# k and v of the later pairs by the seven-product scheme at two levels, q ahead of them, and the attention scale in Wo

## The chip, the core and the metric

The kernel runs on one core of one Trainium2 chip. The core has TensorE (PE, matrix products into PSUM), VectorE (DVE), ScalarE (ACT), GpSimd (POOL) and SyncE (SP), whose queue issues the transfers. Each engine works through its own instructions in a fixed order; a waiting instruction holds up those behind it. The metric is the device time of one execution in microseconds (us).

## The reference, cut to what matters

All tensors are float32. There are 8 sequences of 512 tokens with 512 features.

```python
xn = layernorm(x)                                  # x: (8, 512, 512)
q, k, v = xn @ Wq.T + bq, xn @ Wk.T + bk, xn @ Wv.T + bv
phi_q, phi_k = elu(q) + 1, elu(k) + 1
context = phi_q * cumsum(phi_k * v, axis=tokens) * 32 ** -0.5
s = context @ Wo.T + bo
h = fwht(xn * SU_ug) / 64                          # feed-forward branch, 512 -> 2048 -> 512
a = silu(h @ W_gate.T * w_gate) * (h @ W_up.T * w_up)
d = fwht(a * SU_dp) / 64 @ W_down.T * w_down
out = x + s * silu(d)
```

## The kernel before

**Seven products.** Every matrix product is cut into 2 x 2 blocks and made from seven block products in place of eight. `P1, P2, P7, P3, P4, P5, P6` name the seven factors and their places in a tile. The factors of weights and tokens are sums and differences of blocks (`encode_weights`, `encode_tokens`). A product accumulates in PSUM: bank `px` is read as it grows (after P1, P6, P5 and P3), so each next product into it waits for the reading of the one before; `py` and `pz` hold the others. There are three `px` banks, one `py` and two `pz`, so the next block product starts while the last is still read out.

**Pairs.** Sequences are worked in pairs, `p` = 0 to 3. The token tile `xo` holds 7 outer factors (blocks of sequence and half of the features) by 7 inner ones (again blocks, inside each). `inner_tokens` and `inner_t3` make the inner factors on VectorE. The inner place P7 first holds a plain block and is overwritten by `inner_t3` once the plain blocks are no longer read.

**Two kinds of product.** `group` (line 460 in the helper) applies the scheme once: 7 products of two matrix multiplications of 128x128 by 128x512. `attention` calls it through `project` for k, v and q, twice each (`g`). `block_product` (line 638) is one outer factor of the scheme applied twice: 7 inner products, each two multiplications (the two lanes, gate and up) of 128x128 by 128x256. `hidden_unit` calls it for the 7 outer factors (`outer`) and sums their results on the way: factors P1 and P5 start from nothing and are read out mostly by ScalarE; the other five add an earlier tile, and all seven readings of theirs are on VectorE. Of hidden units there are four per pair (`u`). Pair 0 does its first three by `group` (gate, up), since the weights for the second level have yet to be made.

**Attention.** For each `g`, `attention` makes k, v and q; `elu_plus_one` uses ScalarE twice (Relu, Exp) and VectorE once (line 712); VectorE multiplies v by phi_k (L724), sums over tokens with a scan (L729), and multiplies by phi_q and the scale into the context tile `co` (L737). GpSimd then makes the other factors of `co` (L304 to L307). `project_out` multiplies `co` by Wo after the first hidden unit.

**Weights.** In pair 0 the weights are loaded raw, encoded and stored in DRAM (`keep_w`); `inner_w` makes second-level factors of gate and up from them. Later pairs load stored factors, one tile of 896 KB for each `get_w`, up to three tiles ahead (`ask(3)`, four buffers in `wpool`).

**Order.** `at(place, fn)` puts a step into an agenda whose unit is about one product of two short multiplications; `later(us, fn)` puts work into a queue that `pace` takes out after a reading, up to a given number of microseconds. `background` lowers the priority of what is issued in it. The order on each engine is then fixed ahead of the run by a scheduler.

## Time and profile before

| | |
|---|---|
| timed runs (three) | 1553.84, 1555.47, 1557.9 us; median 1555.47 |
| span of the profiled execution | 1552.4 us (no device time of its own is recorded for it; the median lies 3.1 us above) |
| PE busy | 1523.8 us (98%) |
| PE weight loads busy | 1121.3 us (72%) |
| DVE busy | 1002.4 us (65%) |
| ACT busy | 418.9 us (27%) |
| POOL busy | 436.7 us (28%) |
| moved by DMA | 273.31 MB, 176 GB/s over the span |
| granted PE clock | 0.998 |

"Busy" is the share of the span in which the engine executes something. A matrix multiplication in float32 appears as two records of one half each, so 128 records of a `px` group of k are 64 multiplications. Records of PE are pipelined: the time of one is the distance to the next, not its own length. The profile's page says that spans on GpSimd are rough. In the timeline a row is: start, length, engine, line, operation, output and inputs, count, and in brackets the idle time before it with what ended it.

### The profile page before, as it was taken

The numbers are of one execution on the slowest core, as the hardware profiler recorded it, in microseconds if no ns is written. First come the engines' busy times: TensorE is split into PE (matmuls) and PEld (weight loads), VectorE is DVE, ScalarE is ACT, GpSimd is POOL, SyncE is SP. The second block draws the span as 40 slices with busy tenths as digits, with TensorE's granted clock in tenths as the row PEclk, the third lists the DMA queues.
The fourth block names the chain that finished last, engine by engine and source line by source line (L and its number), as shares of the span: only waits on it lengthen the run. The fifth ranks groups of instructions, "written<-read, shape, count | busy, mean of one in ns | idle before, by whom it ended". The sixth has DMA issues, their size and how long they took to land.

```text
span 1552.4 us, 15693 instructions
## 1 busy us (share of the span) xinstructions
PE 1523.8 (98%) x5924; PEld 1121.3 (72%) x5924; DVE 1002.4 (65%) x1423; ACT 418.9 (27%) x664; POOL 436.7 (28%) x236
## 2 busy tenths in 40 slices
PE   7989999999999999999999999999999999999998
PEld 3436446746874588888884488888886478888887
DVE  7989787378867665516767674715675575533673
ACT  4452341141125411112114431111213431111211
POOL 1232233004320261205511144302621126210631
PEclk9999999999999999999999999999999999999999
DMA  8345877687985244354576344335574233535462
GB/s 276 98 141 176 258 250 240 214 276 261 267 283 162 90 154 160 95 166 164 166 265 235 93 143 149 114 119 186 175 245 155 87 112 102 191 100 174 164 258 81
DMA packets 197692, 273.31 MB, mean 176 GB/s; under 512 B 56816, under 2 KB 155120, under 8 KB 193392
## 3 DMA queue, kind: packets, MB, share of 16 engines
q1 hardware_dynamic: 197472, 272.27, 54.0%
q8 instruction: 47, 0.77, 0.2%
q14 instruction: 29, 0.24, 0.0%
q10 hardware_dynamic: 144, 0.03, 0.0%
HBM read 196.25 MB, written 76.02 MB: 175 GB/s over the span
## 4 chain that ended last, share of the span: by engine, by line
PE 90%; DVE 6%; DMA 1%; ACT 1%; issue 1%; SPq 0%; POOL 0%; POOLq 0%; DVEq 0%; ACTq 0%
PE px_gu L638 20%; PE px_dn L536 13%; PE pz_gu L638 10%; PE pz_dn L536 6%; PE py_gu L638 5%; PE px_k L460 4%; PE py_dn L536 4%; PE px_o L536 3%; PE px_v L460 3%; PE px_q L460 3%; PE px_up L460 2%; PE pz_o L536 2%; PE pz_k L460 2%; PE pz_v L460 2%; PE pz_q L460 2%; PE px_gate L460 1%
## 5 line engine op out<-in xcount | busy, mean ns | idle before, releaser
L638 PE MATMUL px_gu<-xo,w_gu 128*128 128x256 f32 x1456 | 347.7, 380 | 1.4 <-DVE sb_gu L648 1.4
L638 PEld LDWEIGHTS px_gu<-xo,w_gu 128*128 128x128 f32 x1456 | 275.7, 190 | 45.9 <-issue 5.0
L536 PE MATMUL px_dn<-w_down,ho 128*128 128x256 f32 x1024 | 228.7, 379 | 0.0
L536 PEld LDWEIGHTS px_dn<-w_down,ho 128*128 128x128 f32 x1024 | 194.6, 190 | 28.6 <-issue 2.4
L638 PE MATMUL pz_gu<-xo,w_gu 128*128 128x256 f32 x728 | 187.7, 380 | 1.1 <-DVE u L476 1.1
L838 POOL TENSOR_TENSOR u<-u,v 128x1024 f32<-128x1024 f32 x26 | 61.0, 2367 | 365.9 <-DVE u L676 347.4
L638 PEld LDWEIGHTS pz_gu<-xo,w_gu 128*128 128x128 f32 x728 | 137.5, 190 | 22.3 <-DVE u L476 1.5
L536 PE MATMUL pz_dn<-w_down,ho 128*128 128x256 f32 x496 | 112.5, 379 | 1.7 <-DVE u L476 1.7
L536 PEld LDWEIGHTS pz_dn<-w_down,ho 128*128 128x128 f32 x496 | 93.7, 190 | 16.4 <-DVE u L476 2.1
L638 PE MATMUL py_gu<-xo,w_gu 128*128 128x256 f32 x364 | 93.4, 379 | 0.0
L304 POOL TENSOR_TENSOR co<-co 128x512 f32<-128x512 f32 x8 | 14.6, 1829 | 266.3 <-DVE co L737 266.3
L883 POOL TENSOR_TENSOR s<-s,d 128x512 f32<-128x512 f32 x30 | 40.0, 1333 | 165.4 <-ACT d L882 165.4
L638 PEld LDWEIGHTS py_gu<-xo,w_gu 128*128 128x128 f32 x364 | 69.2, 190 | 9.4
L842 POOL TENSOR_TENSOR v<-v,r 128x1024 f32<-128x1024 f32 x26 | 60.9, 2361 | 26.9 <-DVE r L676 26.9
L460 PE MATMUL px_k<-xo,w_k 128*128 128x512 f32 x128 | 61.8, 606 | 0.0
L460 PE MATMUL px_v<-xo,w_v 128*128 128x512 f32 x128 | 60.6, 594 | 0.0
L460 PE MATMUL px_q<-xo,w_q 128*128 128x512 f32 x128 | 60.3, 592 | 0.0
L828 ACT ACTIVATE a<-a,cols_sb 128x512 f32<-128x512 f32 x26 | 18.7, 721 | 149.5 <-DVE a L676 147.8
L882 ACT ACTIVATE d<-d 128x512 f32<-128x512 f32 x31 | 19.5, 630 | 144.4 <-DVE d L551 124.7
L536 PE MATMUL px_o<-w_o,co 128*128 128x256 f32 x256 | 58.2, 379 | 0.0
L828 ACT ACTIVATE u<-u,cols_sb 128x512 f32<-128x512 f32 x52 | 36.9, 720 | 78.2 <-DVE u L676 75.0
L536 PE MATMUL py_dn<-w_down,ho 128*128 128x256 f32 x256 | 57.9, 379 | 0.0
(269 smaller groups left out, 2417.4 us busy)
## 6 DMA issues: line engine op xcount, KB each, us to landing
w_gu<-d_gu SPq DMA_DIRECT2D x91, 896.0 KB, 4.5
w_down<-d_down SPq DMA_DIRECT2D x56, 512.0 KB, 3.8
d_s<-o SPq DMA_DIRECT2D x8, 1024.0 KB, 5.7
d_d<-dn SPq DMA_DIRECT2D x8, 1024.0 KB, 7.7
d<-d_d SPq DMA_DIRECT2D x8, 1024.0 KB, 6.3
s<-d_s SPq DMA_DIRECT2D x8, 1024.0 KB, 8.1
y<-in_x_dram SPq DMA_DIRECT2D x8, 1024.0 KB, 6.4
out_dram<-y SPq DMA_DIRECT2D x15, 512.0 KB, 3.2
```

The lines of the kernel that those rows point to most:

```text
L304: eng.tensor_tensor(o[..., P5, :], o[..., P7, :], o[..., P1, :], ALU.subtract)
L460: nc.tensor.matmul(p.rearrange("p a t -> p (a t)") if len(r.shape) == 2 else p, ws[k][:, i, :], r, start=(first and k == 0), stop=(k == n ...
L536: nc.tensor.matmul(p[:, c], t[:, (2 * g + c) * P : (2 * g + c + 1) * P], ws[i](k), start=(first and k == 0 and c == cs[0]), stop=(k == n - ...
L638: nc.tensor.matmul(p[:, lane], w[:, lane, i, :], x[:, i, :], start=(first and lane == 0), stop=True, skip_group_check=True,)
L828: nc.scalar.activation(g[:, m], g[:, m], AF.Silu, scale=col("w_gate", u + m * NU + a * NG))
L838: nc.gpsimd.tensor_tensor(r[:, m], ru1[:, m], rv[:, m], ALU.add)
L842: nc.gpsimd.tensor_tensor(rv[:, m], rv[:, m], rr[:, m], ALU.add)
L882: nc.scalar.activation(d, d, AF.Silu)
L883: (nc.vector if final and (a, s) == (1, 0) else nc.gpsimd).tensor_tensor(r, r, d, ALU.mult)
```

## The change

Pair 0 is kept, save for the scale. In pairs 1 to 3, `attention_by_blocks` takes the place of `attention`. It first makes q by `group` for both `g`, and writes phi_q into the places P1, P2, P7 and P3 of `co`. It then overwrites the inner P7 blocks (`inner_t3`, which came after all of attention) and makes k and v together as the two lanes of `by_blocks`, which is `hidden_unit`'s sequence of outer factors with what follows taken out as `got`. For each of the four output blocks, `heads` adds the biases and takes the Relu and Exp on ScalarE, ends phi_k on VectorE (`positive`, two of 128x512), multiplies v by phi_k on GpSimd (`weighted`), scans on VectorE (`scan`, two of 128x512), multiplies into `co` on GpSimd (`context`), and makes the other factors of `co` on GpSimd (`sub`). The VectorE steps among them are inserted after readings by `pace`, with 0.9 as its allowance, during k and v and the first hidden unit.

In pair 0, `plain_kv` stores the plain factors of Wk and Wv, and `factors_kv`, hung on the ends of groups 11 to 14, loads the encoded weights again, makes the four second-level factors on VectorE, and stores them. The attention scale goes from L737 into the raw blocks of Wo, multiplied on ScalarE before they are encoded. The later pairs load two tiles for q and seven for k and v, where they loaded six.

```diff
+        elif name[0] == "kv":
+            nc.sync.dma_start(w, inner["kv"][:, name[1]])
...
+    def plain_kv(m, g, w):
+        if "kv" not in inner:
+            inner["kv"] = dram.tile([P, 7, 2, 7, P], F32, tag="d_kv", name="d_kv")
+        d = inner["kv"][:, :, ("k", "v").index(m)]
+        for c, j in ((P1, 0), (P2, 1)) if g == 0 else ((P4, 1),):
+            nc.sync.dma_start(d[:, :, c, :], w[:, j])
+    def factors_kv(m, lo, hi):
+        n = hi - lo
+        t = t8.tile([P, 4, 4, P], F32, tag="t", name=f"f_{m}_{lo}")
+        for g in range(2):
+            nc.sync.dma_start(
+                t[:, 2 * g : 2 * g + 2, :n],
+                kept[f"{m}_{g}"].rearrange("p (j s e) -> p j s e", j=2, s=7)[:, :, lo:hi],
+            )
+        d = inner["kv"][:, lo:hi, ("k", "v").index(m)]
+        def made(c, o, x, y, op):
+            nc.vector.tensor_tensor(t[:, o, :n], t[:, x, :n], t[:, y, :n], op)
+            nc.sync.dma_start(d[:, :, c, :], t[:, o, :n])
+        def make():
+            for c, o, x, y, op in (
+                (P5, 3, 2, 3, ALU.add), (P7, 2, 0, 2, ALU.subtract),
+                (P6, 0, 3, 0, ALU.subtract), (P3, 1, 1, 0, ALU.subtract),
+            ):
+                with background():
+                    made(c, o, x, y, op)
+        at(8, make)
...
-                nc.vector.tensor_tensor(s, px, add[:, m, :, q], ALU.add)
+                pace(nc.vector.tensor_tensor(s, px, add[:, m, :, q], ALU.add), time)
             return s
+        def output(o, s, p):
+            pace(nc.vector.tensor_tensor(o, s, p, ALU.add), time)
...
+    def elu_plus_one(r, name, to=None):
+        neg = t8.tile([P, 2, 2, L], F32, tag="t", name=f"neg_{name}")
+        for h in range(2):
+            nc.scalar.activation(neg[:, h], r[:, h], AF.Relu, scale=-1.0)
+            nc.scalar.activation(neg[:, h], neg[:, h], AF.Exp, scale=-1.0)
+            nc.vector.scalar_tensor_tensor(
+                r[:, h] if to is None else to(h), r[:, h], 1.0, neg[:, h], ALU.add, ALU.max
+            )
...
-                    nc.vector.scalar_tensor_tensor(
-                        co[:, g, h : h + 3 : 2, :], k[:, h], QSCALE, q[:, h], ALU.mult, ALU.mult
-                    )
+                    nc.vector.tensor_tensor(co[:, g, h : h + 3 : 2, :], k[:, h], q[:, h], ALU.mult)
...
+    def attention_by_blocks(p, xo, co, get_w):
+        for g in range(2):
+            def with_q(q, g=g):
+                elu_plus_one(q, f"q_{p}_{g}", lambda h: co[:, g, h : h + 3 : 2, :])
+            project(p, "q", g, xo, get_w, with_q)
+        catch_up()
+        inner_t3(xo, (P1, P5, P6, P2, P7))
+        at(9, lambda: inner_t3(xo, (P3, P4)))
+        made = []
+        def sub(c, a, b):
+            nc.gpsimd.tensor_tensor(co[:, :, c], co[:, :, a], co[:, :, b], ALU.subtract)
+        def heads(t, a, s):
+            k, v = (t[:, :, lane].rearrange("p m q t -> p m (q t)") for lane in range(2))
+            place = (P1, P7, P2, P3)[2 * a + s]
+            neg = co[:, :, (P4, P6, P4, P5)[2 * a + s]]
+            for m in range(2):
+                nc.scalar.activation(
+                    neg[:, m], k[:, m], AF.Relu, bias=nbk[:, m + 2 * a : m + 2 * a + 1], scale=-1.0
+                )
+            nc.scalar.activation(neg, neg, AF.Exp, scale=-1.0)
+            for m in range(2):
+                nc.scalar.activation(v[:, m], v[:, m], AF.Identity, bias=col("bv", m + 2 * a))
+            def positive(m):
+                nc.vector.scalar_tensor_tensor(
+                    k[:, m], k[:, m], bk1[:, m + 2 * a : m + 2 * a + 1], neg[:, m], ALU.add, ALU.max
+                )
+            def scan(m):
+                nc.vector.tensor_tensor_scan(
+                    k[:, m], ones.to_broadcast([P, L]), v[:, m], 0.0, ALU.mult, ALU.add
+                )
+            def weighted():
+                nc.gpsimd.tensor_tensor(v, v, k, ALU.mult)
+                at(4, summed)
+            def summed():
+                for m in range(2):
+                    later(1.2, scan, m)
+                later(0.0, context)
+            def context():
+                nc.gpsimd.tensor_tensor(co[:, :, place], co[:, :, place], k, ALU.mult)
+                made.append(place)
+                if place == P7:
+                    sub(P5, P7, P1)
+                    sub(P6, P3, P5)
+                    sub(P7, P3, P7)
+                if place == P2:
+                    sub(P4, P2, P6)
+            def first():
+                for m in range(2):
+                    later(0.6, positive, m)
+                later(0.0, weighted)
+            at(5, first)
+        by_blocks(p, "kv", xo, lambda i: get_w("kv", i), heads, 0.9)
+        def finish():
+            while len(made) < 4:
+                if not idle and not urgent:
+                    advance(1)
+                catch_up()
+        return finish
...
-    def hidden_unit(p, u, xo, ho, get_w, last):
+    def by_blocks(p, name, xo, weights, got, time=0):
...
-            gated(rv, 1, 1, nc.gpsimd)
+            got(rv, 1, 1)
...
-        outer(P2, ra, ra, lambda: gated(ra, 0, 0, nc.gpsimd))
+        outer(P2, ra, ra, lambda: got(ra, 0, 0))
...
+        outer(P3, rest["u3"], rest["u3"], lambda: got(rest["u3"], 0, 1))
+        outer(P4, ru1, rr, lambda: got(ru1, 1, 0))
+    def hidden_unit(p, u, xo, ho, get_w, last, time=0):
...
+        by_blocks(p, f"gu_{u}", xo, lambda i: get_w("gu", (u, i)), gated, time)
...
+            if m == "o":
+                for raw in (w[:, P1 : P7 + 1], w[:, P4]):
+                    nc.scalar.mul(raw, raw, QSCALE)
             encode_weights(eng, w)
             keep_w(name, t)
+            if m in ("k", "v"):
+                plain_kv(m, g, w)
...
-        queue += [(p, m, g) for g in range(2) for m in ("k", "v", "q")]
+        if p == 0:
+            queue += [(p, m, g) for g in range(2) for m in ("k", "v", "q")]
+        else:
+            queue += [(p, "q", g) for g in range(2)]
+            queue += [(p, "kv", i) for i in (P1, P5, P6, P2, P7, P3, P4)]
...
+    nc.vector.tensor_scalar(nbk, col("bk", 0, KD), -1.0, None, ALU.mult)
+    nc.vector.tensor_scalar(bk1, col("bk", 0, KD), 1.0, None, ALU.add)
...
+    for n, m, lo, hi in ((11, "k", 0, 4), (12, "k", 4, 7), (13, "v", 0, 4), (14, "v", 4, 7)):
+        plan.setdefault(n, []).append(lambda m=m, lo=lo, hi=hi: factors_kv(m, lo, hi))
...
-        attention(p, xo, co, get_w)
-        if p:
-            catch_up()
-            inner_t3(xo, (P1, P5, P6, P2, P7))
-            at(9, lambda: inner_t3(xo, (P3, P4)))
+        heads_made = (attention_by_blocks if p else attention)(p, xo, co, get_w)
...
-                hidden_unit(p, u, xo, ho, get_w, u % 2 == 1)
+                hidden_unit(p, u, xo, ho, get_w, u % 2 == 1, 0.9 if u == 0 else 0)
                 if u == 0:
+                    heads_made()
                     project_out(p, co, get_w)
```

## The prediction

> **What bounds the kernel now.** I read the page's first part, the chain that ended last, and the windows by stage; then the timeline of single engines at the places that the change touches.

> ```profile
> span 1552.4 us, 15693 instructions
> PE 1523.8 (98%) x5924; PEld 1121.3 (72%) x5924; DVE 1002.4 (65%) x1423; ACT 418.9 (27%) x664; POOL 436.7 (28%) x236
> PE 90%; DVE 6%; DMA 1%; ACT 1%; issue 1%; SPq 0%; POOL 0%; POOLq 0%; DVEq 0%; ACTq 0%
> ```

> TensorE carries 90% of the chain. Windows show where it idles: columns are PE, PEld, DVE, ACT and POOL busy, clock, DMA share, GB/s.

> ```profile
> 240.00:260.00 20.00, 18.29 (x70) 13.01 (x69) 15.21 (x19) 1.17 (x2) 10.31 (x5) 1.00 0.68 200
> 457.00:530.00 73.00, 73.00 (x178) 33.07 (x177) 49.56 (x64) 32.91 (x41) 7.11 (x6) 1.00 0.50 155
> 530.00:572.00 42.00, 42.00 (x190) 35.57 (x189) 30.86 (x44) 14.11 (x19) 20.48 (x11) 1.00 0.43 138
> ```

> The second is attention of pair 1, the third its first hidden unit: TensorE is never idle. Only work taken off TensorE, or a new wait of TensorE, moves the time there. The idle time lies in pair 0 and at both ends. The next rows, TensorE's timeline at 522 us, give the price of a product: the distance between starts, since lengths overlap.

> ```profile
> 522.67 1.88 PE L460 MATMUL pz_q<-xo,w_q 128*128 128x512 f32 x4
> 524.39 1.88 PE L460 MATMUL px_q<-xo,w_q 128*128 128x512 f32 x4
> 526.11 1.03 PE L638 MATMUL px_gu<-xo,w_gu 128*128 128x256 f32 x4
> 526.97 1.03 PE L638 MATMUL py_gu<-xo,w_gu 128*128 128x256 f32 x4
> ```

> A product of two multiplications (four records) costs 1.717 us 512 wide and 0.863 us 256 wide.

> **TensorE.** Removed per later pair: k and v, four groups of 7 products, 28 x 1.717 = 48.1 us. Added: 7 outer factors of 7 products, 49 x 0.863 = 42.3 us. That is 5.8 us less, 17.4 us for three pairs. Weight loads double for the same columns but stay covered: 190 ns each beside 216 ns between starts, and hidden units already run so.

> **VectorE in the same stretch.** The prices are starts of neighbouring readings (541.49, 542.09), 0.60 us for 128x512; half of the 128x1024 row of L712, 0.60, for one `positive`; half of the two scans in 2.33, 1.16, for a `scan`. Before, k and v of a pair took 12 readings (7.2), twelve operations of 128x1024 at 1.14 (13.7) and 8 scans (9.3): 30.2 us beside 48.1 of TensorE. After: 41 readings (24.6), 8 `positive` (4.8), 8 scans (9.3): 38.7 beside 42.3. The total fits, but not evenly. A block is done only after outer factors P2, P7, P3 and P4, so all 16 inserted operations come late. In the order that the scheduler fixes for the changed kernel they lie between the first readings of outer P3 and the sixth product of the hidden unit's fourth outer factor. There are 34 readings (20.4) and 16 insertions (14.1) there, 34.5 us, against 42 products, 36.2 us. VectorE is 95% booked before it waits for anything.

> **What it waits for.** GpSimd gets 16 operations of 128x1024 per pair (rows of L838, L829: 2.36 us each) where `co` had 8 of 128x512 (1.27): +27.6 us. Some 10 of them fall in that stretch, 25 us of about 42, busy some 60%. These rows show what becomes of two engines that both read SBUF:

> ```profile
> 69.07 5.93 POOL L305 TENSOR_TENSOR co<-co 128x512 f32<-128x512 f32 x1
> 74.97 1.72 POOL L307 TENSOR_TENSOR co<-co 128x512 f32<-128x512 f32 x1
> 74.39 1.17 DVE L939 TENSOR_TENSOR r_gate<-r_gate 128x512 f32<-128x512 f32 x1
> 75.48 1.76 DVE L940 TENSOR_TENSOR r_gate<-r_gate 128x512 f32<-128x512 f32 x1
> 537.69 2.19 POOL L304 TENSOR_TENSOR co<-co 128x512 f32<-128x512 f32 x1 [28.34 <-DVE co L737]
> 539.26 1.70 DVE L737 SCALAR_TENSOR_TENSOR co<-k,q 128x1024 f32<-128x1024 f32 x1
> 98.00 6.01 DVE L729 TENSOR_TENSOR_SCAN k<-ones,v 128x512 f32<-128x512 f32 x4
> 563.64 4.69 POOL L842 TENSOR_TENSOR v<-v,r 128x1024 f32<-128x1024 f32 x2 [2.13 <-DVE r L676]
> 565.40 0.69 DVE L648 TENSOR_TENSOR sc_gu<-px_gu,u 128x512 f32<-128x512 f32 x1 [0.17 <-PE px_gu L638]
> ```

> L305 needed 5.93 us in place of 1.27 while VectorE went through SBUF operations without a gap. L940 needed 1.76 in place of 0.68: it stood until L307 ended at 76.69. The multiplication at 539.26 took 1.70, not 1.22, and GpSimd's operation ended 0.62 after it began. Four scans beside GpSimd took 6.01 us, not 4.66. But a reading out of PSUM (565.40) keeps its 0.69 beside GpSimd. So hidden units did not pay; `positive` and `scan`, inserted where GpSimd runs, will, and readings queued behind them stand too. TensorE waits for these, since the next product into `px` needs the last reading.

> On the price: 16 insertions, 60% of them meeting a running operation, with half of 2.36 left of it: 16 x 0.6 x 1.18 = 11.3 us. VectorE then needs 34.5 + 11.3 = 45.8 us in 36.2, 9.6 short. TensorE tolerates some lag: around 539 us VectorE ran two inserted multiplications (1.22 and 1.70) and TensorE lost some 0.3. I allow 2, which leaves about 7.6.

> [...]

> **ScalarE's queue.** `heads` puts instructions that wait for GpSimd ahead of readings. Count from when the last product of outer P7 has been issued. VectorE has its result 1.6 us later; GpSimd, which started `weighted` of the block before at 0.4 and ends it at 2.8, makes its two sums until 7.5. ScalarE's second Relu of that block starts then. Behind it come a bias, the Exp, and Relu and bias of the next block: 4 x 0.57 (starts of neighbours at 480.64 and 481.21) and 0.97 (474.27 and 475.24), to 10.8. Only then does it read the hidden unit's first `px`, to 11.4. TensorE wants that bank ten products later, at 8.6. It loses 2.8 us, whatever the lock does; part of VectorE's lag is worked off meanwhile. I take 8 us per pair for both. The bounds: 1 (insertions fall into gaps, ScalarE's wait is met by other products) and 12 (strict turns).

> Old stalls that go: a later pair lasted 363.2 us (820.2 less 457.1, first products of k) against 361.9 of products; 0.3 lies at the old handover to the hidden unit, 0.9 in three pairs. `inner_t3` moves ahead of k and v with the same seven operations (0.42 us) and the same wait, for the end of q: nothing. ScalarE's table loads stay as many (23; 1.28 us each where uncovered). Multiplying by phi_q without the scale is one input's arithmetic less: nothing.

> **Pair 0.** 16 operations of VectorE (0.60 or less, 9 us), in windows from 220 to 300 us with 34 us of VectorE idle: hidden there. Transfers: 6 stores of 448 KB early, then 8 loads and 16 stores, 7.2 MB. At 295 GB/s, the most that the window 180 to 200 us moved with all engines busy, that is 24 us; in 200 to 300 us the DMA share leaves 27 idle. It just fits. SP's queue is in order, so stores that wait for VectorE stand ahead of the raw loads of gate and of `w_down`, and at 240 to 260 us TensorE already lost 1.7 with a weight load as releaser. Bounds 0 and 10, nearest to that row: 2. Weights of later pairs: +2.7 MB each at 6 us per tile of 896 KB, the pace of hidden units, whose transfers land in 4.5: nothing. Scaling Wo is four ScalarE operations off the chain: nothing.

> **Sum.** -17.4 + 3 x 8 - 0.9 + 2 = +7.7 us. The span becomes 1560.1; the median lies 3.1 above the span, so 1563.2.

> **The rivals.**
> *The insertions mostly find gaps (faster).* VectorE's readings come every 0.863 us and take 0.60, GpSimd may slip between them, and the lag is absorbed; ScalarE's 2.8 us stay, with 0.4 more: -17.4 + 9.6 - 0.9 + 2 = -6.7, 1548.8. For it: TensorE lost only 0.3 at 539 us. Against: 60% of GpSimd's time is taken. It decides below 3.8 us of loss per pair.
> *Full gain.* ScalarE's wait is covered too, 0.5 us per pair: -14.8, 1540.7. Against it stands the order of its queue.
> *Break-even.* Loss of 3.8 to 7 us per pair: 1550.6 to 1560.2; at 5.4, 1555.4.
> *Pair 0 pays more.* Loads come late behind the added transfers, 10 in place of 2: 1571.2.

> **How the numbers follow.** A measurement here can tell about 0.3%, 4.7 us, from no change. Forecast (loss over 7 us per pair) 0.45; pair 0 besides 0.12; break-even 0.18; insertions in gaps 0.17; full gain 0.08. Slower is 0.45 + 0.12, rounded 0.57; same 0.18; faster 0.25. The range leaves out the full gain and the upper half of the case with pair 0: 1546 to 1576, where 12 us per pair gives 1575. The likeliest case alone is 1560 to 1576.

> **What would show it.** Right: per pair, TensorE's products last 5.8 us less, but the first products of two successive pairs stand about 365 us apart, not 363; TensorE waits at the start of the first hidden unit for ScalarE's `sa_gu` and VectorE's readings; scans show means well above 1.16 us, and GpSimd's `co` products above 2.36. Wrong: pairs of 358 to 360 us, scans at 1.16, no wait at that handover. A TensorE idle time between 200 and 400 us that grows by more than 5 us would put the loss in pair 0.

## The result, and the profile after

The changed kernel takes 1599.98 us, the median of four runs (1593.7 to 1602.12), against 1554.65 for the kernel before beside it: a ratio of 1.0285, 95% interval 1.0261 to 1.0309. It is slower, by 45 us, outside the range that was given. The profiled execution is the fastest of the four (1593.7, span 1591.9).

The page of the changed kernel, its first part and the chain:

```profile
span 1591.9 us, 16438 instructions
PE 1526.9 (96%) x6176; PEld 1176.0 (74%) x6176; DVE 1064.3 (67%) x1516; ACT 419.1 (26%) x680; POOL 525.0 (33%) x260
PE 69%; DVE 5%; issue 2%; DMA 2%; POOL 1%; SPq 1%; ACT 1%; POOLq 0%; DVEq 0%; ACTq 0%
```

TensorE's share of the chain falls from 90% to 69%. Its busy time has not fallen although its products are shorter, largely because some ran at half clock, as shown below.

Where the time went is read from landmarks on TensorE's timeline, the first product of each pair. In the profiled execution pair 1 begins at 469.78 us (before 457.07), pair 2 at 841.81 (820.23). So pair 0 lost 12.7 us, where 2 were predicted, and a later pair takes 372.0 us, where 363.2 were taken and 365 predicted.

Pair 1 by windows (after the length, the columns as before: PE, PEld, DVE, ACT, POOL, clock, DMA share, GB/s). The first window holds q and most of k and v, the second their end and the first hidden unit:

```profile
470.00:534.00 64.00, 64.00 (x241) 45.28 (x240) 49.39 (x74) 26.59 (x36) 12.05 (x7) 1.00 0.65 204
534.00:592.00 58.00, 48.40 (x201) 39.45 (x200) 48.51 (x58) 19.03 (x28) 42.68 (x18) 0.94 0.37 116
```

All of the 9.6 us that TensorE idles in pair 1 lie in the second, beside VectorE at 84% and GpSimd at 74%. Four of its waits there, from TensorE's timeline:

```profile
540.42 0.70 PE L676 MATMUL px_gu<-xo,w_gu 128*128 128x256 f32 x2 [3.58 <-ACT sa_gu L684]
...
557.55 1.99 PE L676 MATMUL px_gu<-xo,w_gu 128*128 128x256 f32 x8 [1.26 <-DVE sa_gu L686]
561.10 1.13 PE L676 MATMUL pz_gu<-xo,w_gu 128*128 128x256 f32 x4 [1.55 <-DVE v_gu L690]
569.56 2.07 PE L676 MATMUL px_gu<-xo,w_gu 128*128 128x256 f32 x4 [2.09 <-DVE sc_gu L686]
```

The first is the forecast wait for ScalarE's reading; the others are VectorE's lag. The timelines of ScalarE, GpSimd and VectorE ahead of it:

```profile
533.16 0.72 ACT L811 ACTIVATE co<-v_kv,nbk 128x512 f32<-128x512 f32 x1 [7.89 <-POOL v_kv L943]
539.81 0.56 ACT L684 COPY sa_gu<-px_gu 128x512 f32<-128x512 f32 x1
528.45 2.36 POOL L829 TENSOR_TENSOR a_kv<-a_kv 128x1024 f32<-128x1024 f32 x1 [7.87 <-DVE a_kv L819]
530.76 5.60 POOL L943 TENSOR_TENSOR v_kv<-v_kv,r_kv 128x1024 f32<-128x1024 f32 x2
537.59 2.35 POOL L838 TENSOR_TENSOR co<-co,a_kv 128x1024 f32<-128x1024 f32 x1 [1.23 <-DVE a_kv L824]
531.80 2.41 DVE L824 TENSOR_TENSOR_SCAN a_kv<-ones,a_kv 128x512 f32<-128x512 f32 x1
534.71 2.73 DVE L824 TENSOR_TENSOR_SCAN a_kv<-ones,a_kv 128x512 f32<-128x512 f32 x1
538.78 2.38 DVE L819 SCALAR_TENSOR_TENSOR v_kv<-v_kv,bk,co 128x512 f32<-128x512 f32 x2 [0.75 <-ACT co L814]
```

ScalarE stands 7.89 us for GpSimd's sums (L943), which stand behind `weighted` (L829). VectorE's scans, inserted into the same stretch, take 2.41 and 2.73 us, not 1.16, and two `positive` 2.38, not 1.20, each beside one of GpSimd's operations from 528.45 to 536.36 and from 537.59 to 539.94 us. All this is as the prediction had it. What it had not is in the next rows, windows of 2 us after the first wait:

```profile
540.00:542.00 2.00, 0.89 (x3) 0.49 (x4) 2.00 (x4) 0.58 (x2) 0.70 (x1) 1.00 0.00 0
542.00:544.00 2.00, 2.00 (x6) 1.55 (x6) 1.55 (x3) 2.00 (x3) 1.67 (x1) 0.52 0.00 0
```

The clock column falls to 0.52 once the wait is over. TensorE is busy all of 542 to 544 us, but with 6 records where 9 or 10 fit at 0.216 us each. The clock records of this trace hold six such stretches in the three later pairs, 23.9 us in all at half clock, so up to 12 us of work lost, 4 per pair. The kernel before has none there. What sets them off is worked out in the last section.

### The profile page after: what moved, and what is told of

Read it like the earlier page. It is cut to its first block, busy times and chain, and to the rows that moved or that the text cites. A ratio compares the mean times of both kernels' runs of the same rounds, so it can differ in the third digit from the quotient of the medians.

```text
span 1591.9 us, 16438 instructions
## 1 busy us (share of the span) xinstructions
PE 1526.9 (96%) x6176; PEld 1176.0 (74%) x6176; DVE 1064.3 (67%) x1516; ACT 419.1 (26%) x680; POOL 525.0 (33%) x260
## 4 chain that ended last, share of the span: by engine, by line
PE 69%; DVE 5%; issue 2%; DMA 2%; POOL 1%; SPq 1%; ACT 1%; POOLq 0%; DVEq 0%; ACTq 0%
PE px_gu L676 17%; PE px_dn L574 11%; PE pz_gu L676 9%; PE pz_dn L574 5%; PE py_gu L676 4%; PE px_kv L676 4%; PE py_dn L574 3%; PE px_o L574 3%; PE px_q L498 3%; PE pz_kv L676 2%; PE pz_o L574 1%; PE pz_q L498 1%; SPq L237 1%; POOL v_kv L943 1%; PE py_kv L676 1%
## 5 line engine op out<-in xcount | busy, mean ns | idle before, releaser
L676 PE MATMUL px_gu<-xo,w_gu 128*128 128x256 f32 x1456 | 354.8, 384 | 24.1 <-ACT sa_gu L684 10.7
L676 PEld LDWEIGHTS px_gu<-xo,w_gu 128*128 128x128 f32 x1456 | 277.4, 192 | 71.0 <-ACT sa_gu L684 11.9
L676 PE MATMUL pz_gu<-xo,w_gu 128*128 128x256 f32 x728 | 192.3, 388 | 7.3 <-DVE v_gu L690 4.7
L939 POOL TENSOR_TENSOR u_gu<-u_gu,v_gu 128x1024 f32<-128x1024 f32 x26 | 61.0, 2369 | 347.1 <-DVE u_gu L717 334.4
L676 PEld LDWEIGHTS pz_gu<-xo,w_gu 128*128 128x128 f32 x728 | 140.2, 194 | 31.0 <-DVE v_gu L690 6.1
L676 PE MATMUL py_gu<-xo,w_gu 128*128 128x256 f32 x364 | 93.4, 379 | 0.0
L676 PE MATMUL px_kv<-xo,w_kv 128*128 128x256 f32 x336 | 82.5, 386 | 0.1
L676 PEld LDWEIGHTS py_gu<-xo,w_gu 128*128 128x128 f32 x364 | 69.2, 190 | 9.4
L676 PEld LDWEIGHTS px_kv<-xo,w_kv 128*128 128x128 f32 x336 | 65.2, 195 | 14.6 <-issue 3.6
L943 POOL TENSOR_TENSOR v_gu<-v_gu,r_gu 128x1024 f32<-128x1024 f32 x26 | 60.9, 2363 | 20.6 <-DVE r_gu L717 20.4
L915 POOL TENSOR_TENSOR ho<-g,u 128x512 f32<-128x512 f32 x6 | 12.9, 2152 | 153.6 <-DVE u L514 153.6
L966 ACT ACTIVATE a_gu<-a_gu,cols_sb 128x512 f32<-128x512 f32 x26 | 18.7, 721 | 169.4 <-DVE a_gu L717 167.8
L966 ACT ACTIVATE u_gu<-u_gu,cols_sb 128x512 f32<-128x512 f32 x52 | 36.9, 720 | 78.2 <-DVE u_gu L717 75.0
```

Of the source, the lines that this page charges most:

```text
L676: nc.tensor.matmul(p[:, lane], w[:, lane, i, :], x[:, i, :], start=(first and lane == 0), stop=True, skip_group_check=True,)
L915: nc.gpsimd.tensor_tensor(ho[:, P1], g[:, 0, 0], r[:, 0, 0], ALU.mult)
L939: nc.gpsimd.tensor_tensor(r[:, m], ru1[:, m], rv[:, m], ALU.add)
L943: nc.gpsimd.tensor_tensor(rv[:, m], rv[:, m], rr[:, m], ALU.add)
L966: nc.scalar.activation(g[:, m], g[:, m], AF.Silu, scale=col("w_gate", u + m * NU + a * NG))
```

## The experiments

Beside each the kernel before ran on the same chip, and a difference to it is to its median there. That median lay between 1553.77 and 1556.44, so a difference between two versions that ran on different chips is uncertain by some 3 us. "Per pair" is the distance between the first products of pairs 1 and 2 in the profile.

### Pair 0 alone, later pairs alone

`pair0_only`: the changed kernel with the old attention in all pairs, so that the new weights are made and not read; Wo is still scaled.

```diff
-            queue += [(p, "q", g) for g in range(2)]
-            queue += [(p, "kv", i) for i in (P1, P5, P6, P2, P7, P3, P4)]
...
+        queue += [(p, m, g) for g in range(2) for m in ("k", "v", "q")]
...
-        heads_made = (attention_by_blocks if p else attention)(p, xo, co, get_w)
+        attention(p, xo, co, get_w)
```

> The kernel before with the additions of pair 0 alone: its weights' extra factors are made and stored, and nothing reads them; q, k and v of all pairs are computed as before. By the traces the first product of pair 1 comes 12.7 us later than before in the changed kernel. Theory (the transfers of pair 0 and their place in SP's queue cost that): about 1567 us, 12.7 above the kernel before, pairs 363.2 us apart, the loss between 220 and 450 us with a DMA share near 0.9. Rival (pair 0 lost most of that to chance, a slow clock after a wait that the kernel before has too): 1555 to 1559.

Measured: 1570.79, 15.5 above before, ratio 1.0101 (1.0086 to 1.0116). Pair 1 starts at 474.3 us, pairs are 363.3 apart. So pair 0 alone costs 15 us.

`later_only`: the changed kernel without `plain_kv` and `factors_kv`; the later pairs load stored factors of gate and up for k and v, which have other values by it.

```diff
-            nc.sync.dma_start(w, inner["kv"][:, name[1]])
+            nc.sync.dma_start(w, inner[0][:, name[1]])
...
-            if m in ("k", "v"):
-                plain_kv(m, g, w)
...
```

> The changed kernel without the additions of pair 0; the later pairs take the gate and up factors of hidden unit 0 as weights of k and v, so k and v have other values, with the same instructions and bytes. Theory (the two losses add up): 12.7 us less than the changed kernel, about 1587, pairs 372 us apart. Rival (the loss in the later pairs hangs on a late arrival out of pair 0): below 1575.

Measured: 1595.79, only 4 below the changed kernel. Pairs are 372.7 apart, but pair 1 starts at 471.2 us: pair 0 loses 14 us although no factor is made. Both expectations fail, and the theory that the transfers cost pair 0 its time falls with them. Two suspects were left in pair 0: the scaling of Wo, and whatever else the change leaves there.

A chain through three queues spoke for Wo. The DMA queue of the kernel before, then that of `later_only` with VectorE and TensorE:

```profile
118.65 0.33 SPq L326 DMA_DIRECT2D d_o<-w_o  x1
130.53 6.89 SPq L354 DMA_DIRECT2D w_up<-in_wup_t_dram  x8
```

```profile
128.29 0.33 SPq L328 DMA_DIRECT2D d_o<-w_o  x1
133.19 5.44 SPq L358 DMA_DIRECT2D w_up<-in_wup_t_dram  x8
139.78 0.69 DVE L1049 TENSOR_TENSOR r_up<-w_up 128x512 f32<-128x512 f32 x1 [3.50 <-DMA w_up<-in_wup_t_dram]
141.72 3.62 PE L574 MATMUL pz_o<-w_o,co 128*128 128x256 f32 x8 [3.45 <-DVE g L514]
```

GpSimd encodes Wo only when ScalarE has scaled it, and by then the context's subtractions stand in front. The store of Wo is issued 9.6 us later, the loads of `w_up` behind it 2.7 us later, VectorE waits 3.5 us for them, and an unrelated reading behind that wait holds TensorE.

### The parts of pair 0

`wo_scale_only` is the kernel before with this alone (and the scale taken out of the product with phi_q):

```diff
+            if m == "o":
+                for raw in (w[:, P1 : P7 + 1], w[:, P4]):
+                    nc.scalar.mul(raw, raw, QSCALE)
```

> The kernel before with one part of the change: Wo is scaled by ScalarE when it is loaded, and the product with phi_q carries no scale. No factors for k and v are made. The runs so far lose 12 to 17 us in pair 0 with and without those factors, and in all of them GpSimd encodes the second Wo tile only after the context's eight subtractions, since it waits for ScalarE's scaling: the tile's store then stands 10 us longer in SP's queue, and the raw loads of w_up behind it come 2.7 us late, on which VectorE waits 3.5 us and TensorE 3.5. Theory (the scaling, through two queues, is most of the loss in pair 0): first product of pair 1 at 466 to 471 us in place of 457.1; 1564 to 1570. Rival (the extra transfers and tiles are the loss): 1554 to 1558.

Measured: 1558.49, 2.8 above before, ratio 1.0020 (1.0010 to 1.0031). The chain is there (TensorE waits 3.3 us for g), but it is worth 3 us, not 10. (Its profile, in which pair 1 starts at 464.2 us, is of the slowest of its ten runs.)

`factors_only` is the kernel before with `plain_kv` and `factors_kv` called as in the change.

> The kernel before with the other part of pair 0's additions alone: the factors of k and v are made and stored (7.2 MB, 16 operations of VectorE) and not read; the scale stays in the product with phi_q, Wo is as before. Theory (scaling of Wo is most of the loss): 1555 to 1562, first product of pair 1 at 458 to 463 us, no wait of 3.5 us for g near 141 us. Rival (the transfers are the loss): 1566 to 1572.

Measured: 1557.39, 1.7 above before, ratio 1.0013 (1.0001 to 1.0025). The added transfers, 10.1 MB in all (283.40 against 273.31; the prediction's 7.2 and its six early stores), cost the 2 us that the prediction gave them.

`v_scaled` is the changed kernel with the scale in ScalarE's bias addition, for which it keeps a scaled bias in one more constant tile:

```diff
+    bvq = const.tile([P, KD], F32, tag="bvq", name="bvq")
...
-                nc.scalar.activation(v[:, m], v[:, m], AF.Identity, bias=col("bv", m + 2 * a))
+                nc.scalar.activation(
+                    v[:, m], v[:, m], AF.Identity, bias=bvq[:, m + 2 * a : m + 2 * a + 1], scale=QSCALE
+                )
...
```

> The changed kernel with the scale of attention in another place: in pair 0 in the product with phi_q as before, in the later pairs in ScalarE's addition of the bias to v (an activation that is there anyway), and not in Wo. Theory (the scaling of Wo costs pair 0 some 8 to 12 us through the queues of GpSimd and SP): 1588 to 1593, later pairs unchanged at 372 us. Rival (pair 0 loses to the transfers): 1598 to 1602.

Measured: 1600.01, no gain. The parts sum to 4.5 us, and whole versions lose 12 to 17. The only thing left that the losing kernels have and these two parts lack is a pair of constant tiles of 16 bytes per partition, `nbk` and `bk1`; `v_scaled` has a third, `bvq`, so it was no clean test of Wo's scaling.

`before_shifted` adds only these to the kernel before:

```diff
+    nbk = const.tile([P, KD], F32, tag="nbk", name="nbk")
+    bk1 = const.tile([P, KD], F32, tag="bk1", name="bk1")
     su_dp = const.tile([P, NF], F32, tag="su_dp", name="su_dp")
...
+    nc.vector.tensor_scalar(nbk, col("bk", 0, KD), -1.0, None, ALU.mult)
+    nc.vector.tensor_scalar(bk1, col("bk", 0, KD), 1.0, None, ALU.add)
```

> The kernel before with nothing of the change but two small constant tiles (nbk and bk1, 128x4 each) and the two operations that fill them; nothing reads them. They stand ahead of all large tiles, so every large SBUF tile lies 64 bytes further: xo at byte 20032 of its partition, not 19968 (a multiple of 512), and the rest with it. Every run so far with these two tiles lost 12 to 17 us in pair 0 (with the factors, without them, with and without the scaling of Wo); the two without them lost 2 to 3. In the former the mean packet of 128 bytes took 17 to 20 us in the trace's units against 13.0 in the latter. Theory (the place of the tiles slows the transfers of pair 0): 1563 to 1570, first product of pair 1 at 465 to 473 us, 13.0 becomes 16 to 20. Rival (chance of the order in pair 0; the tiles don't matter): 1554 to 1558.

Measured: 1565.87, 12.1 above before, ratio 1.0079 (1.0064 to 1.0094); pair 1 starts at 466.7 us. `after_aligned` is the test from the other side, the changed kernel with the two tiles in the last pool:

```diff
-    nbk = const.tile([P, KD], F32, tag="nbk", name="nbk")
-    bk1 = const.tile([P, KD], F32, tag="bk1", name="bk1")
...
+    nbk = small.tile([P, KD], F32, tag="nbk", bufs=1, name="nbk")
+    bk1 = small.tile([P, KD], F32, tag="bk1", bufs=1, name="bk1")
```

> The changed kernel with nbk and bk1 at the end of SBUF, so that all large tiles lie where they lie in the kernel before. Same instructions. Theory (the shift by 64 bytes costs pair 0 some 9 us): 1588 to 1593, first product of pair 1 at 459 to 464 us, later pairs 372 us apart. Rival (it doesn't matter): 1598 to 1602.

Measured: 1588.27, 11.7 below the changed kernel (10.8 when each is held against its own kernel before); pair 1 starts at 464.6 us, pairs are 372.2 apart. Same instructions, another address. Which transfers feel it is seen in the list of DMA issues (count, KB each, median us to landing), first of the kernel before, then of `before_shifted`, then of `after_aligned`:

```profile
z<-d_x SPq DMA_DIRECT2D x24, 256.0 KB, 4.7
```

```profile
z<-d_x SPq DMA_DIRECT2D x24, 256.0 KB, 6.1
```

```profile
z<-d_x SPq DMA_DIRECT2D x24, 256.0 KB, 5.2
```

`z` is loaded in packets of 128 bytes. Their mean duration is 13.0 or 13.1 ns in each run whose tiles lie where they did before and 16.4 to 19.6 in each run with the tiles in front. It is a part of them that is slow: in `before_shifted` 28% take more than 13 ns, in the kernel before 0.2%. The raw loads of gate go from 2.9 to 3.7 us in `before_shifted`, and VectorE's waits for raw gate and up weights from 5.5 to 12.9 us in all. That the place of the tiles makes the 12 us is shown; by what step inside the transfers is not.

How the loads reach TensorE shows in pair 0, first of the kernel before, then of `before_shifted`:

```profile
0.00:457.07 457.07, 434.22 (x1388) 262.17 (x1389) 362.30 (x538) 152.71 (x287) 119.69 (x81) 1.00 0.71 226
0.00:466.71 466.71, 440.56 (x1389) 266.23 (x1390) 357.03 (x540) 153.10 (x287) 121.94 (x81) 0.98 0.72 221
```

Of the 9.6 us between these two profiles 3.3 are more idle time of TensorE and 6.3 are longer busy time for the same products: it ran at half clock for 20.5 us, against 3.4 before. All four runs of `before_shifted` show a granted clock of 0.992 to 0.994, the kernel before beside them 0.997 or more, which is some 6 us.

`aligned_v_scaled` takes the scale out of Wo as `v_scaled` did, at the old addresses.

> As the last, and the scale of attention goes into ScalarE's bias addition of v (later pairs) and the product with phi_q (pair 0) in place of Wo, which costs no instruction. Theory (scaling Wo holds up GpSimd's and SP's queues for some 3 us): 1585 to 1590, 3 less than the run beside it. Rival (nothing): the same as the run beside it.

Measured: 1584.91, 3.4 less than `after_aligned`, as expected. This is the base of the experiments that follow; its pairs are 373.4 us apart.

### The later pairs

`products_on_vector` was made on the changed kernel itself:

```diff
-                nc.gpsimd.tensor_tensor(v, v, k, ALU.mult)
+                nc.vector.tensor_tensor(v, v, k, ALU.mult)
...
-                nc.gpsimd.tensor_tensor(co[:, :, place], co[:, :, place], k, ALU.mult)
+                nc.vector.tensor_tensor(co[:, :, place], co[:, :, place], k, ALU.mult)
```

> The changed kernel with the two products of each block (phi_k times v, and the prefix sum times phi_q) on VectorE in place of GpSimd, as inserted operations of 1.2 us. VectorE gets 9 us more per pair, GpSimd 19 less. [...]

Measured: 1599.61, the same as the changed kernel. The mean of the scans falls (by group from 2.20, 2.57 and 1.21 us to 1.21, 1.96 and 1.21), but the 9 us of added work cost as much as that gained. The time lies between the author's two estimates: 1577 to 1592 with scans of 1.2 to 1.8 us, 1610 to 1627 with the 9 us on top.

`products_left_out` leaves both lines out.

> The changed kernel without the two products of each block: v isn't weighted by phi_k, and the context keeps phi_q alone. VectorE has the same work as in the changed kernel, GpSimd 8 operations of 2.36 us less per pair. Theory (the turns with GpSimd and ScalarE's queue behind GpSimd's sums are the loss): scans near 1.2 to 1.8 us, a later pair loses 2 to 6 us in place of 14.7: 1562 to 1575. Rival (VectorE's own 34.5 us in 36.2 are too many, whatever GpSimd does): 1593 to 1600.

Measured: 1578.47; 366.6 us per pair, and no half clock in the later pairs. By the profiles 5.4 of the 14.7 us go, by the times (21.5 us less) some 7 per pair, a little outside the expected range. That is not the turns alone: TensorE's wait for `sa_gu` falls with them from 3.58 to 1.55 us.

`hold_removed` puts ScalarE's steps of one block later:

```diff
+            def on_scalar():
...
-            at(5, first)
+            if (a, s) == (1, 1):
+                at(9, on_scalar)
+            else:
+                on_scalar()
```

> The changed kernel with ScalarE's five instructions for the block that waits for GpSimd's sums (Relu, Relu, Exp and the two biases of v) put into its queue nine products later, and what follows them with them; the reading sa_gu of the first hidden unit no longer stands behind them. Nothing else differs. Theory: the wait of 3.6 us for sa_gu goes and with it the half clock that follows it (1.7 us), while VectorE's lag is the next wait: 2 to 4 us less per pair, 1588 to 1594. Rival (VectorE is late anyway and the wait only changes its name): 1598 to 1602.

Measured: 1618.29, 18 worse. It was not the clean cut that the expectation claims: the block now comes after its successor, so two differences of the context tile are taken before it is finished and hold other values, and GpSimd's subtractions meet VectorE's last insertions. The timelines of GpSimd and VectorE there:

```profile
564.68 8.64 POOL L804 TENSOR_TENSOR co<-co 128x1024 f32<-128x1024 f32 x3
562.68 5.22 DVE L822 SCALAR_TENSOR_TENSOR u_kv<-u_kv,bk,co 128x512 f32<-128x512 f32 x2
```

Two `positive`, 1.40 us when alone, take 5.22 beside them, and TensorE waits 7.0 us for a reading behind. As a test of the hold it is inconclusive.

`kv_first` computes k and v ahead of q, so that the insertions should fall into the 24 us of q ("the last" in its expectation is `aligned_v_scaled`). For that the products with phi_q move from GpSimd to VectorE, and `inner_t3` runs seven operations more per pair. Its edit, of which this is the order alone:

```diff
...
-            queue += [(p, "q", g) for g in range(2)]
             queue += [(p, "kv", i) for i in (P1, P5, P6, P2, P7, P3, P4)]
+            queue += [(p, "q", g) for g in range(2)]
```

> The last, with k and v computed ahead of q in the later pairs, so that the block-wise operations that VectorE has inserted (positive, scan) fall into the 24 us of q, in which it has only 8 us of its own, and not into the first hidden unit; the reading of the first hidden unit no longer stands behind ScalarE's steps for the blocks. The scans write into the context tile, phi_q is multiplied in afterwards on VectorE as in the kernel before. The inner sums of the tokens are made in the down product of the pair before; place P7 of them is turned back for q and again for the hidden units (7 more operations of 0.4 us). Theory (the place of the inserted work is the loss): a later pair takes 357 to 361 us, 1545 to 1556 in all. Rival (VectorE is overloaded wherever it falls): 368 to 372 us per pair, 1580 to 1590.

Measured: 1584.86, the same as its base; 374.7 us from pair 1 to pair 2. The theory fails; the time is in the rival's range, the pair is 3 us above it. VectorE is busy without a gap from 500 to 516 us and again from 530 to 550, TensorE waits 3.6 us for `sc_kv` in the first and 1.1 to 1.3 us three times from 543 to 554. Since VectorE got more work too, the run does not part the place of the work from its amount.

The next four take the work on finished blocks away step by step, from `aligned_v_scaled`. `heads_left_out`:

```diff
         def heads(t, a, s):
...
-            for m in range(2):
-                nc.scalar.activation(neg[:, m], ...)
...
-            at(5, first)
+            at(12, encoded)
```

> The aligned kernel with the scale in v, and in the later pairs without everything that is done to a finished block of k and v: no Relu, Exp and biases on ScalarE, no positive and scan on VectorE, no products on GpSimd; the context tile keeps phi_q and its four sums. What is left of the new scheme is its products, 41 readings per pair and GpSimd's inner sums. Theory (all of the loss per pair comes from the work on the blocks): 357 to 359 us per pair, 1539 to 1546. Rival (the readings and GpSimd's inner sums alone already hold TensorE up): over 361 us per pair, 1552 or more.

Measured: 1540.0, ratio 0.9898 (0.9883 to 0.9913). Pair 1, TensorE's busy time in the first column after the length:

```profile
462.00:819.00 357.00, 357.00 (x1597) 302.53 (x1596) 217.25 (x319) 76.73 (x112) 114.14 (x53) 1.00 0.54 174
```

TensorE is never idle, and the pair takes 357.0 us: 6.2 less than before, where the prediction's 5.8 and 0.3 make 6.1. The scheme on TensorE does what it should, and its 41 readings fit.

`insertions_left_out` keeps ScalarE's steps.

> As the last, but with ScalarE's steps (Relu, Exp, biases) kept; VectorE's positive and scan and GpSimd's products are left out, so VectorE has readings alone. ScalarE's steps of one block wait for GpSimd's inner sums, which begin 1.2 us earlier here than in the changed kernel. Theory (ScalarE's queue holds the reading sa_gu some 2 us, the rest is VectorE with GpSimd): 359 to 361 us per pair, 1545 to 1553. Rival (ScalarE's queue is the larger half): 364 to 368, 1562 or more.

Measured: 1541.00, 358.4 us per pair, a little below the theory's ranges. With ScalarE's steps alone TensorE waits 0.55 us for `sa_gu`. The wait of 3.58 us needs the work of GpSimd: in the next two runs it is 1.56 us without GpSimd's products and 0.67 without its sums as well.

`products_left_out_2` keeps VectorE's insertions too and leaves out GpSimd's products alone; `gpsimd_silent` leaves out its inner sums of k and v as well.

> The aligned kernel with the scale in v, without GpSimd's two products of each block (v isn't weighted by phi_k, the context keeps phi_q alone); all else is kept, VectorE's 16 insertions too. The same part was left out earlier in the kernel with the shifted tiles: 366.6 us per pair. Theory (half of the loss is the turns with those products): 366 to 367 us per pair, 1562 to 1568. Rival (the earlier run was bettered by chance): 1575 or more.

> As the last, and GpSimd's inner sums of k and v are taken away too: one block is copied by ScalarE in place of being summed, the other stays without its sum. From the first block to the first hidden unit's own sums GpSimd is silent but for four subtractions on the context; VectorE has all its readings, positive and scan. [...] Rival (VectorE's own work is too much beside TensorE's products): 364 to 367 us per pair, 1560 or more.

Measured: 1566.58 and 366.1 us per pair, as expected; then 1560.49 and 364.8, both at the low end of the rival's ranges. The author's other estimate for `gpsimd_silent`, 1541 to 1552 with scans near 1.16 us, was missed. The rival is not shown by it, since GpSimd's four subtractions stayed and still lengthen VectorE's work. Timelines of VectorE and GpSimd in `gpsimd_silent`:

```profile
526.20 1.22 DVE L826 TENSOR_TENSOR_SCAN a_kv<-ones,a_kv 128x512 f32<-128x512 f32 x1
543.15 3.07 DVE L821 SCALAR_TENSOR_TENSOR u_kv<-u_kv,bk,co 128x512 f32<-128x512 f32 x2
546.75 3.07 DVE L826 TENSOR_TENSOR_SCAN u_kv<-ones,u_kv 128x512 f32<-128x512 f32 x1
542.65 2.37 POOL L804 TENSOR_TENSOR co<-co 128x1024 f32<-128x1024 f32 x1 [6.63 <-DVE u_kv L821]
546.39 2.35 POOL L804 TENSOR_TENSOR co<-co 128x1024 f32<-128x1024 f32 x1 [1.38 <-DVE u_kv L821]
```

Alone a scan takes 1.22 us. Where a subtraction is under way (542.65 to 545.02, 546.39 to 548.74), what VectorE begins meanwhile ends later by nearly the rest of the subtraction: a scan 3.07 in place of 1.22, two `positive` 3.07 in place of 1.40.

`thin_2` keeps all work and inserts after every second reading only.

```diff
+    def spread(ins, us):
...
+            pace(ins, 0.1 if readings[0] % 2 == 0 else 0)
```

> The aligned kernel with the scale in v, all work kept, with one inserted operation after every second reading of VectorE, not after every one: the 16 insertions of a pair then lie over some 52 readings, 45 us of TensorE, and not over 38. Theory (VectorE falls behind because 34.5 us of work and 11 us of turns stand in 36 us; over 45 us it needs some 53): half of the lag goes, 366 to 370 us per pair, 1566 to 1578. Rival (each turn stops TensorE by itself, wherever it falls): 1583 to 1588.

Measured: 1578.24, 6.7 less than its base (8.8 when each is held against its own kernel before), 370.3 us per pair, half clock 10.2 us in place of 30.7. Just outside the expected range, at its dear end.

`thin_2_sums` moves GpSimd's two late sums to VectorE.

```diff
-                nc.gpsimd.tensor_tensor(rv[:, m], rv[:, m], rr[:, m], ALU.add)
+                (nc.vector if name == "kv" else nc.gpsimd).tensor_tensor(rv[:, m], rv[:, m], rr[:, m], ALU.add)
```

> As the last, with GpSimd's two inner sums of the block that ScalarE waits for moved to VectorE (2 x 1.14 us there, 5.6 us less on GpSimd), so that ScalarE's steps start some 3 us earlier and sa_gu isn't held. Theory: the wait of 3.6 us for sa_gu and the half clock behind it go, VectorE's 2.3 us cost less than that: 2 to 4 us per pair less than the run beside it, 1556 to 1572. Rival (VectorE is the bound, the hold is hidden in its lag): 2 us per pair more than the run beside it.

Measured: 1595.32, 17 worse than `thin_2`; 377.2 us per pair. `sa_gu` is held longer than in `thin_2` (2.3 us against 1.4), and `sa_kv` 2.4 us: worse than either theory. VectorE has no room for 2.3 us more at that place.

No version that computes all of k and v by the new scheme beat the kernel before; the best of them, `thin_2`, is 1.5% slower (1.0132 to 1.0170).

## Why the prediction was wrong

The mechanism in the later pairs was right, and slower was the likeliest case; the loss per pair was taken too small, one cost was set at nothing, and one does not appear in the sum. The forecast fell 37.6 us short (7.7 against 45.3): some 21.6 of that are the loss per pair, 14.6 pair 0.

- **TensorE, -17.4 and -0.9.** Right. Without the work on blocks a pair takes 357.0 us against 363.2; three times 6.2 is 18.6, where 18.3 were forecast.
- **Pair 0, +2.** The term itself, the transfers, was right: 1.7 us (interval 0.2 to 3.9). What was missing are two costs outside it. "Scaling Wo is four ScalarE operations off the chain: nothing" failed: 2.8 us (3.4 taken out again at the old addresses). The step followed ScalarE alone and not GpSimd's queue, in which the scaled tile's encoding waits, nor SP's queue behind that. And the two constant tiles, which shift every tile behind them, are nowhere in the prediction: 12.1 us, the largest part of the loss in pair 0, about half of it as half clock. 1.7 + 2.8 + 12.1 = 16.6, and `pair0_only` lost 15.5.
- **The loss, 8 us per pair.** Mis-sized: 372.2 less 357.0 is 15.2. Taking the profiles of `aligned_v_scaled`, `products_left_out_2`, `gpsimd_silent`, `insertions_left_out` and `heads_left_out` in this order (373.4 us per pair in the first), the steps are 7.2 for GpSimd's products (2.6 of them idle time of TensorE, 9.3 to 6.7, and 4.6 busy time, 364.1 to 359.4, which is mainly the half clock), 1.3 for its sums, 6.4 for VectorE's insertions (with what they take longer beside GpSimd's subtractions, 3.07 us in place of 1.22 or 1.40), 1.4 for ScalarE's steps. The hold of ScalarE's queue was forecast as 2.8 us and measured as 3.58. The bound of 12 had no place for half clock, which took up to 4 per pair and goes away together with GpSimd's products. The prediction gives no sum for that bound, and its own terms do not make it: with all 16 insertions paying 1.18 us, 34.5 + 18.9 less 36.2 and the 2 allowed is 15.2. No run shows turns at all 16 insertions, or what the prediction calls the lock; in their place the runs showed some operations of VectorE that ended later beside a running one of GpSimd, two `positive` and a scan by 1.67 and 1.85 us in `gpsimd_silent`. Nor does the measured 15.2 confirm that sum, since half clock and ScalarE's steps are in it; what is shown is that 8, and the bound of 12, were too small.
- **The sum again,** with measured terms: -18.6 + 3 x 15.2 + 16.6 = 43.6 us, against 45.3 measured. The loss per pair in it is the difference of two pair lengths, so this tests the parts of pair 0, and the loss only by its parts above.
- **What would show it.** Scans above 1.16, the wait for `sa_gu` and the longer pair all came as listed, and TensorE's idle time between 200 and 400 us grew from 8.0 to 15.4, so that line pointed to the right stage; but the rival for pair 0 named the added transfers as the cause, and these were not it.

What stays open: how the 6.4 us divide between VectorE's own 14 us of insertions and their lengthening beside four subtractions, how much of the half clock would have been idle time in any case, and by what step a tile's address slows its transfers.

## What to carry to other kernels

Before costing a new constant tile at nothing, look up which tiles come behind it in SBUF and whether their addresses move, here from multiples of 512 bytes to 64 beyond one, for 12.1 us; put small new tiles last. Where two engines that read SBUF are both busy in a stretch (here 84% and 74%), look at every meeting: a scan of 1.22 us took 3.07 beside one GpSimd operation. Add up TensorE's waits in windows of 3.4 us, since waits that lie together cost half clock besides, small ones too (here 1.34 and 1.08 us, 2.28 of idle time in one window). Separate a change's parts early and look for what all losing versions share: here it was not the part that moved 10 MB.

## What the runs showed of the hardware

A shift of all large SBUF tiles by 64 bytes, from multiples of 512, made packets of 128 bytes slower (13.0 to 16.4 ns on average with nothing else changed) and cost this kernel 12.1 us of 1554.

TensorE's clock fell to one half for 3.41 or 6.83 us (once 10.24) after waits, but the length of one wait does not tell when. In the changed kernel half clock followed the waits of 3.58 and of 2.09 us at 540 and 569 us. In `thin_2_sums` it did not follow one of 2.27 us at 542 us, and in `kv_first` it followed one of 1.08 us at 554 us. A wait of 3.7 us near 103 us in pair 0, for ScalarE's `w_gate`, is followed by it in some of these kernels and not in others, the kernel before among the latter.

```profile
101.46:104.87 3.41, 1.43 (x4) 0.36 (x2) 3.12 (x3) 0.25 (x1) 1.46 (x1) 1.00 0.34 145
104.87:108.28 3.41, 1.68 (x4) 0.87 (x5) 0.93 (x3) 3.39 (x8) 0.00 (x0) 1.00 1.06 345
550.89:554.30 3.41, 1.13 (x4) 0.68 (x4) 3.41 (x5) 0.00 (x0) 2.19 (x2) 1.00 0.87 233
```

In the kernel before the wait is split by the grid, 1.98 and 1.74 us of idle time fall into the two windows, and the clock stays full. In `kv_first` two waits add up to 2.28 us in one window, and half clock begins at its end. In all 20 traces (the first 20 us and the last 4 left out) a window at full clock with more than 2.0 us idle was followed by half clock each time, 91 of 91; of those with less than 1.86 us, over 8800, none was; between the two it went either way, 10 of 27. So in these traces the grid decided whether a wait of 2 to 4 us brought half clock: in the changed kernel the wait near 103 us, 3.71 long, has 2.23 us in one window, and half clock follows from 105.16 us.
